# Rearranging the first rounds of a two-layer graph kernel: count reads, a cast, attention logits and a row written to HBM

## The chip, the cores and the metric

The kernel runs on one core of one Trainium2 chip. The metric is device time in microseconds (us) from launch to the end of the kernel. A core has engines that work side by side, each with its own in-order list of instructions: TensorE (PE, matrix products into PSUM), VectorE (DVE), ScalarE (ACT), GpSimd (POOL). SyncE (SP) only issues transfers (DMA), also in order; the transfers themselves run on the core's DMA engines.

## The reference, cut to what matters

The input is a graph of 3327 nodes with 64 features each and a dense 0/1 adjacency matrix. There are two layers, each with a layer norm in front and a residual behind.

```python
# layer 0: attention over hyperbolic log maps
x_t = logmap0(x, c)
left, right = x_t @ w_att[:D, 0], x_t @ w_att[D:, 0]
adj_att = sigmoid(left[:, None] + right[None, :] + b_att[0]) * adj
x_local = logmap(x[:, None, :], x[None, :, :], c)
support_t = einsum('ij,ijd->id', adj_att, x_local)
return proj(expmap(x, support_t, c), c)
...
# layer 1: the last 100 neighbours of each node, weights halving with the rank
rank = cumsum(mask, axis=1); deg = rank[:, -1:]
k = minimum(deg, 100.0); pos = rank - (deg - k)
w = mask * where(pos > 0, 0.5 ** (k - pos), 0.0)
return w @ (input @ weight) + bias
```

Both layers need the adjacency matrix. The kernel reads it once: while layer 0 runs over it, it also counts for each edge how many neighbours lie behind it, and keeps that as small integers for layer 1.

## The kernel before, in words

The nodes are padded to 26 blocks of 128. The output nodes are cut into four strips of 8, 8, 6 and 4 blocks (`STRIPS`), worked in the order blocks 18 to 25, 10 to 17, 4 to 9, 0 to 3. Within a strip, **rounds** go over the 26 source blocks from the last to the first, one block per round in the first three strips and two in the last: 91 rounds in all. A round handles a tile of up to 128 x 1024 pairs.

The work of a round is spread over the engines, and the order of instructions on PE, DVE, ACT and POOL is the order of the program text (`manual_schedule`, line 681). Transfers that SyncE issues are not in that list; their order on the SyncE queue is fixed when the program is built, by the framework. In round n of the loop at line 1173:

- `total` (line 672): PE adds the attention-weighted features of round n-2 into `po`.
- ACT runs two Gelu passes over the pair products `pq` of round n (lines 1190, 1191).
- DVE multiplies the attention by the adjacency (line 1197, the **first product**), which needs the Tanh of round n (line 655) and the adjacency tile `ad`.
- `edges` (line 622): DVE makes the 0/1 mask of round n+3 from its adjacency tile.
- `count` (lines 633, 634): PE adds the mask of round n+2 to running counts in `pc`. There is one `pc` buffer, so a count waits until the one before has been read.
- ACT computes the Tanh of round n+1 (`sigmoids`, line 655).
- `read` (lines 644 to 648): the counts of round n+2 are clipped and written to SBUF, by ACT or by DVE. `ON_ACT` gives the share of ACT, in the first strip every second one, and the first two are always ACT's.
- `products` (lines 662, 663): PE makes the pair products of round n+1. There are two `pq` buffers in PSUM; a new tile waits for the second product of the tile that had its buffer.
- DVE forms the **second product** (line 1214), which needs the Gelu results of round n.

Adjacency tiles have five buffers (`ADB`). The load for round n+4 stands at the head of round n and can start when the first product of round n-1 has let its buffer go.

Before the loop only the node data of blocks 18 to 25 (`first`) are prepared. Those of blocks 0 to 17 (`others`) are made by the generator `second_group`, one step at the end of each of the first rounds, in rounds 0 to 7. Its steps touch: the features `zf` (line 718), a half-precision cast of them on ACT (line 882), the remainder on DVE (line 885), two transposing transfers to `ju` and `jz` (lines 886, 887), logarithms on ACT with their table loads (line 890 and `logarithms`), `artanh` on DVE, and `logits`: 36 small matmuls (line 768) into a tile that takes a turn in the two `pq` buffers, then three DVE instructions (769 to 771). At line 895 the 128 x 18 values of `left` go to an HBM row `left_d`, one 4-byte value at a time; each later strip reads its part of this row, broadcast to 128 partitions, into `left_b` (line 588). While `second_group` still has a step, the loop skips what follows at line 1216, among it the small `range_steps`.

Of the kernel before, what the change touches and what calls it, by code (L numbers as in the profile page):

```python
# [11 lines left out]
F32 = mybir.dt.float32  # L12
# [10 lines left out]
P = 128  # L23
N = 3327
NB = 26
# [5 lines left out]
JD = range(12, 16)  # L31
IN_ORDER = {mybir.EngineType.PE, mybir.EngineType.DVE, mybir.EngineType.Activation, mybir.EngineType.Pool}
AHEAD = 2
SGB, ADB = 5, 5
ON_ACT = ((1, 2), (5, 8), (3, 4), (1, 2))

# [409 lines left out]
def fast(ctx, tc, x, adj_t, r, w_att, b_att, weight, bias, out, flag):  # L446

    nc = tc.nc
# [188 lines left out]
    def read(n, j):  # L637
        k, lo, hi = rounds[n]
        S = strips[k]
        kept = behind(j)[:, S.i0 : S.i0 + S.F]  # L640
        num, den = ON_ACT[k]
        i = NB - 1 - j
        if (n < AHEAD and k == 0) or i * num // den != (i + 1) * num // den:
            A.activation(kept, S.pc[:, : S.F], AF.Relu, scale=128.0 if j in JD else 1.0)  # L644
        elif j in JD:
            V.tensor_scalar(kept, S.pc[:, : S.F], 0.0, 128.0, op0=ALU.max, op1=ALU.mult)
        else:
            V.tensor_scalar(kept, S.pc[:, : S.F], 0.0, None, op0=ALU.max)  # L648
# [16 lines left out]
    def total(n):  # L665
        k, lo, hi = rounds[n]
        S = strips[k]
        if hi == NB:
            S.po = ps.tile([P, FMAX], F32, name="po")
        for j in js(n):  # L670
            for f0, f1 in S.hv:
                T.matmul(S.po[: D + 1, f0:f1], hw[:, j, :], part(n, sg_of[n], j, f0, f1),  # L672
                         start=j == NB - 1, stop=j == 0)
# [23 lines left out]
    zf = d  # L697
# [64 lines left out]

    def logits(bs, tag, bufs):

        plr = ps.tile([P, NB, 2], F32, name=tag, bufs=bufs)
        for b in range(bs.start, bs.stop):
            for part in (0, 1):
                T.matmul(plr[:, b, :], jz[:, b, :], w_h[:, part], start=part == 0, stop=part == 1)
        V.tensor_mul(left[:, bs], plr[:, bs, 0], yr[:, bs])
        V.tensor_mul(right[:, bs], plr[:, bs, 1], yr[:, bs])  # L770
        V.tensor_scalar(right[:, bs], right[:, bs], batt, 0.5, op0=ALU.add, op1=ALU.mult)

    A.activation(load_table, one_c, AF.Ln)
    centred(first)
# [50 lines left out]
    logarithms(first)  # L825
    read(0, NB - 1)
    artanh(first)
    logits(first, "po", 1)
    products(0)
    summing_table(first)  # L830
    pl = first_left()
# [3 lines left out]
    pq = pq_of[0]  # L835
# [11 lines left out]
    def second_group():  # L847

        o = others
        A.activation(rl[:, o], d[:, o], AF.Relu)  # L850
        V.tensor_reduce(ss[:, o], sq2, AX.X, ALU.add)
        V.tensor_scalar(v[:, o], ss[:, o], 1.0 / D, EPS_LN, op0=ALU.mult, op1=ALU.add)
        guess(V, yt[:, o], y[:, o], v[:, o])
        newton(V, yt[:, o], y[:, o], v[:, o], 3)
        A.activation(sr2, rl[:, o], AF.Square)
        yield
        V.tensor_reduce(rs[:, o], sr2, AX.X, ALU.add)
        V.tensor_mul(x2[:, o], y[:, o], y[:, o])
        V.tensor_mul(x2[:, o], x2[:, o], rs[:, o])
        V.tensor_scalar(bal[:, o], x2[:, o], negc, 1.0, op0=ALU.mult, op1=ALU.add)  # L860
        V.scalar_tensor_tensor(babs[:, o], bal[:, o], -1.0, bal[:, o], op0=ALU.mult, op1=ALU.max)
        V.reciprocal(nrm[:, o], babs[:, o])
        V.scalar_tensor_tensor(yz[:, o], nrm[:, o], zs_c, y[:, o], op0=ALU.mult, op1=ALU.mult)

        nz2 = pre.tile([P, n2, D], F32, name="sq2").bitcast(F16).rearrange("p b (c d) -> p b c d", c=2)
        nu2 = pre.tile([P, n2, D], F32, name="sr2").bitcast(F16)
        G.memset(nu2[:, :, KB + 6 :], 0.0)
        G.memset(nu2[:, :, D + 6], -WB * QS)
        G.memset(nu2[:, :, KB + 6], 1.0)
        G.tensor_scalar(as_[:, o], x2[:, o], za_c, None, op0=ALU.mult)  # L870
        the_rest(o, nu2, nu2, KB)
        G.tensor_scalar(x2c[:, o], x2[:, o], MIN_NORM, None, op0=ALU.max)
        t = yt[:, o]
        G.tensor_tensor(yr[:, o], x2c[:, o], nhalf, op=ALU.pow)
        G.tensor_mul(t, yr[:, o], yr[:, o])
        G.tensor_mul(t, t, x2c[:, o])
        G.tensor_scalar(t, t, -0.5, 1.5, op0=ALU.mult, op1=ALU.add)
        G.tensor_mul(yr[:, o], yr[:, o], t)
        clipped(G, o)
        yield  # L880
        features(o)
        A.copy(nz2[:, :, 0], zf[:, o])
        V.tensor_copy(nu2[:, :, :D], zf[:, o])
        yield
        V.tensor_sub(nz2[:, :, 1], zf[:, o], nz2[:, :, 0])
        nc.sync.dma_start_transpose(ju[:, o], nu2.rearrange("p b f -> p (b f)"))
        nc.sync.dma_start_transpose(jz[:, o], nz2.rearrange("p b c d -> p (b c d)"))
        summing_table(o)
        yield
        A.activation(load_table, one_c, AF.Ln)  # L890
        logarithms(o)
        yield
        artanh(o)
        logits(o, "pq", 2)
        nc.sync.dma_start(left_d.rearrange("(b p) -> p b", p=P)[:, o], left[:, o])
        yield
        V.tensor_scalar(balm, bal, MIN_NORM, None, op0=ALU.max)
        V.reciprocal(sk, balm)
        G.tensor_scalar(ih, babs, 2 / WA, None, op0=ALU.mult)
        G.tensor_scalar(w2s, w2, 2.0**27 / HS, None, op0=ALU.mult)  # L900
        G.tensor_mul(su, nrm, balm)
        G.tensor_mul(sv, bal, su)
        G.tensor_scalar(sk, sk, sqc, None, op0=ALU.mult)
        G.tensor_scalar(maxnorm, absr, 1.0 - EPS_BALL, None, op0=ALU.mult)
        G.tensor_mul(c2_c, c_c, c_c)
        G.tensor_scalar(m2c, c_c, -2.0, None, op0=ALU.mult)
        G.tensor_scalar(p2c, c_c, 2.0, None, op0=ALU.mult)
        yield
        ahead.close()

        behind_of["lo"] = ctx.enter_context(tc.tile_pool(name="lo", bufs=1, side="right", reuse_waits="tile")).tile(
            [P, JD.start, NP], U8, name="behind_lo")


    def range_steps():
        t1 = post_pool.tile([P, NB], F32, name="st1")
        V.tensor_mul(t1, nrm, node)
        V.tensor_reduce(st[:, 0:1], t1, AX.X, ALU.max)
        yield 2
        V.scalar_tensor_tensor(t1, x2, c_c, t1, op0=ALU.mult, op1=ALU.mult)  # L920
        V.tensor_reduce(st[:, 1:2], t1, AX.X, ALU.max)
        yield 2
        V.tensor_mul(t1, bal, node)
        V.tensor_reduce(st[:, 2:3], t1, AX.X, ALU.max)
        yield 2
        V.tensor_reduce(st[:, 3:4], t1, AX.X, ALU.min)
        V.tensor_scalar(st[:, 3:4], st[:, 3:4], -1.0, None, op0=ALU.mult)
# [237 lines left out]
    def finish():  # L1165
# [2 lines left out]
                pass  # L1168
        stages.clear()

    stages, rest_of_ahead = [Stage(range_steps())], second_group()
    range_end = in_range()
    for n in range(R):
        k, lo, hi = rounds[n]
        m, w = n + AHEAD, span(n)
        ended, turned = (n > i and rounds[n - i - 1][1] == 0 for i in (1, 2))
        if m + 2 < R:
            if rounds[m + 2][2] == NB:
                strip_in(rounds[m + 2][0])
            load(m + 2)  # L1180
        two = m < R and len(js(m)) == 2
        if two:
            count(m, js(m)[0])
        if turned:
            pa = turn(k - 1)
        elif n > 1:
            total(n - 2)
        pq = pq_of.pop(n)[:, :w]
        if n > 0:
            A.activation(pq, pq, AF.Gelu, scale=-WG / QS)  # L1190
            A.activation(pq, pq, AF.Gelu, scale=WH)  # L1191
        asked_of_act()
        if turned:
            finish()
            stages.append(Stage(per_node(k - 1, pa)))
        sg = sg_of[n][:, :w]
        V.scalar_tensor_tensor(sg, sg, 1.0, ad_of.pop(n)[:, :w], op0=ALU.add, op1=ALU.mult)  # L1197
        if m + 1 < R:
            edges(m + 1)
        if two:  # L1200
            read(m, js(m)[0])
        if m < R:
            count(m, js(m)[-1])
        if n + 1 < R:
            sigmoids(n + 1)
        if m < R:
            read(m, js(m)[-1])
        if ended:
            strip_out(k - 1)
        if 0 < n < R - 1:  # L1210
            products(n + 1)
        if hi - lo > 1:
            advance(PORTIONS[k])
        V.scalar_tensor_tensor(sg, pq, WD, sg, op0=ALU.add, op1=ALU.mult)  # L1214
        if next(rest_of_ahead, True) is None:
            continue
        advance(PORTIONS[k])
        if turned:
            total(n - 2)
        if n > R - 3:  # L1220
            next(range_end)
# [135 lines left out]
```

## Time and profile before

The time before is 434.22 us, the median of three runs (432.78 to 435.92). The profiled execution spans 433.1 us, with a mean granted TensorE clock of 0.956.

| engine | busy us | share of the span |
|---|---|---|
| TensorE (PE) | 369.5 | 85% |
| VectorE (DVE) | 382.3 | 88% |
| ScalarE (ACT) | 364.4 | 84% |
| GpSimd (POOL) | 137.4 | 32% |

The profile is one execution as the hardware profiler records it. Its timeline lists instructions with start, duration, engine and line, and how long the engine had stood idle and for whom. Busy durations of neighbours on one engine overlap a little, so the distance from one start to the next, the pitch, is the better price in a full queue. A round of the first strip costs, by pitch, on DVE 1.13 + 0.62 + 1.13 us (first product, mask, second product) and 1.13 more if DVE reads the counts; on ACT 1.03 + 0.92 + 1.05 us (two Gelu, Tanh) and 0.91 more if ACT reads them.

| first product of round | starts at, us | | round | starts at, us |
|---|---|---|---|---|
| 0 | 25.82 | | 7 | 69.97 |
| 1 | 34.13 | | 8 | 73.14 |
| 2 | 40.06 | | 9 | 80.95 |
| 3 | 46.16 | | 10 | 85.96 |
| 4 | 51.02 | | 11 | 90.23 |
| 5 | 55.03 | | 12 | 93.10 |
| 6 | 62.41 | | 13 | 97.09 |

### The profile page before, as it was taken

How to read it: one execution, taken by the hardware profiler on the slowest of the kernel's cores; microseconds unless marked ns; L12 is line 12 of the kernel's file. 1: busy time of each engine (PE TensorE's matmuls, PEld its weight loads, DVE VectorE, ACT ScalarE, POOL GpSimd, SP SyncE). 2: the span in 40 equal slices, each digit the busy share in tenths (PEclk: the TensorE clock that was granted, in tenths of full speed). 3: DMA queues.
4: the chain of work that ended last, by engine and by line, in shares of the span. 5: the costliest groups of instructions: out<-in, count | busy, mean ns of one | idle time of the engine just before them, and what ended most of it. 6: DMA issues, size and time to landing. Idle time of an engine off the chain costs nothing.

```text
span 433.1 us, 4690 instructions
## 1 busy us (share of the span) xinstructions
PE 369.5 (85%) x1423; PEld 153.1 (35%) x1423; DVE 382.3 (88%) x550; ACT 364.4 (84%) x412; POOL 137.4 (32%) x267
## 2 busy tenths in 40 slices
PE   0485679799999899999999899999787999898883
PEld 0241223233333333333333344444332333343352
DVE  6899976699999989999999898899998999898851
ACT  3495796699999989999999989999897899787620
POOL 6504932000000017581024062850223284253400
PEclk9998888899999999999999899999998999999888
DMA  6612677744455535544444444544543330000012
GB/s 197 179 49 68 155 170 46 196 147 146 145 152 184 169 107 151 177 145 141 123 128 139 145 119 137 148 118 137 173 147 106 110 98 0 0 2 0 1 26 63
DMA packets 32252, 50.28 MB, mean 116 GB/s; under 512 B 17877, under 2 KB 18307, under 8 KB 32218
## 3 DMA queue, kind: packets, MB, share of 16 engines
q1 hardware_dynamic: 29050, 49.07, 40.3%
q10 hardware_dynamic: 2976, 0.75, 0.8%
q8 instruction: 13, 0.21, 0.2%
q14 instruction: 21, 0.17, 0.1%
q0 software_dynamic: 192, 0.07, 0.1%
HBM read 46.40 MB, written 0.86 MB: 109 GB/s over the span
## 4 chain that ended last, share of the span: by engine, by line
DVE 29%; ACT 28%; PE 17%; issue 11%; DMA 10%; POOL 2%; ACTq 0%; POOLq 0%; SPq 0%; DVEq 0%
ACT sg L655 9%; DVE sg L1214 8%; ACT pq L1190 8%; DVE sg L1197 6%; PE po L672 6%; ACT pq L1191 4%; DMA x_sb<-in_x 4%; DMA left_d<-left 3%; ACT behind_lo L644 3%; DMA ad<-in_adj_t 2%; DVE behind_lo L648 2%; DVE wt L1245 2%; ACT behind_hi L644 2%; PE pc L633 2%; PE pq L663 2%
## 5 line engine op out<-in xcount | busy, mean ns | idle before, releaser
L672 PE MATMUL po<-sg,hw 128*65 128x512 f32 (+1 forms) x364 | 167.3, 585 | 0.4 <-DVE st L938 0.4
L1214 DVE SCALAR_TENSOR_TENSOR sg<-pq,sg 128x1024 f32<-128x1024 f32 (+1 forms) x91 | 104.1, 1144 | 9.5 <-ACT pq L1191 9.0
L1197 DVE SCALAR_TENSOR_TENSOR sg<-sg,ad 128x1024 f32<-128x1024 f32 (+1 forms) x91 | 104.7, 1151 | 0.4 <-ACT sg L655 0.3
L655 ACT ACTIVATE sg<-left_b,right 128x1024 f32<-128x1024 f32 (+2 forms) x103 | 99.4, 978 | 0.0
L1190 ACT ACTIVATE pq<-pq 128x1024 f32<-128x1024 f32 (+1 forms) x90 | 86.1, 956 | 8.8 <-PE pq L663 8.4
L1191 ACT ACTIVATE pq<-pq 128x1024 f32<-128x1024 f32 (+1 forms) x90 | 85.2, 946 | 2.9
L633 PE MATMUL pc<-mask,ca 128*128 128x512 bf16 (+1 forms) x175 | 65.1, 372 | 22.4 <-DVE behind_hi L648 7.5
L672 PEld LDWEIGHTS po<-sg,hw 128*65 128x65 f32 x364 | 51.1, 143 | 73.7 <-issue 59.9
L662 PE MATMUL pq<-iu,ju 71*128 71x512 f16 (+1 forms) x182 | 69.7, 383 | 2.2 <-DVE yr L526 0.8
L663 PE MATMUL pq<-iz,jz 128*128 128x512 f16 (+1 forms) x182 | 68.2, 382 | 1.4 <-DMA iz<-nz 1.4
L634 PE MATMUL pc<-mask,cb 128*128 128x512 bf16 (+1 forms) x182 | 66.3, 375 | 1.5 <-DVE sg L1214 1.5
L622 DVE TENSOR_SCALAR mask<-ad 128x1024 bf16<-128x1024 f32 (+1 forms) x91 | 59.5, 654 | 5.1 <-DMA ad<-in_adj_t 5.1
L634 PEld LDWEIGHTS <-cb 128*128 128x128 bf16 x182 | 18.0, 99 | 64.9 <-issue 54.1
L1010 POOL TENSOR_TENSOR dots<-dots,ih 128x8 f32<-128x8 f32 (+1 forms) x3 | 2.6, 873 | 119.3 <-DVE dots L1030 119.3
L1257 PE MATMUL pw<-wt,s 128*128 128x512 bf16 (+1 forms) x154 | 35.6, 388 | 5.1 <-DVE s L1115 2.5
L662 PEld LDWEIGHTS <-ju 71*128 71x128 f16 x182 | 18.3, 100 | 29.2 <-DVE sg L1214 7.9
L633 PEld LDWEIGHTS <-ca 128*128 128x128 bf16 x175 | 17.5, 100 | 30.8 <-issue 19.0
L1257 PEld LDWEIGHTS <-s 128*128 128x128 f16 x182 | 18.4, 103 | 26.1 <-issue 7.1
L1010 POOL TENSOR_SCALAR t<-t 128x8 f32<-128x8 f32 (+1 forms) x9 | 6.3, 702 | 63.7 <-DVE t L1104 63.2
L663 PEld LDWEIGHTS <-jz 128*128 128x128 f16 x182 | 18.4, 101 | 19.2 <-issue 3.4
L644 ACT ACTIVATE behind_lo<-pc 128x1024 uint8<-128x1024 f32 (+2 forms) x29 | 24.9, 858 | 0.0
L644 ACT ACTIVATE behind_hi<-pc 128x1024 uint8<-128x1024 f32 (+2 forms) x24 | 20.7, 863 | 3.4 <-PE pc L634 3.4
(324 smaller groups left out, 389.4 us busy)
## 6 DMA issues: line engine op xcount, KB each, us to landing
ad<-in_adj_t SPq DMA_DIRECT2D x65, 512.0 KB, 3.5
ad<-in_adj_t SPq DMA_DIRECT2D x26, 384.0 KB, 3.1
out<-o SPq DMA_DIRECT2D x6, 128.0 KB, 2.0
x_sb<-in_x ACTq DMA_DIRECT2D x1, 576.0 KB, 15.9
left_b<-left_d SPq DMA_DIRECT2D x1, 512.0 KB
left_b<-left_d SPq DMA_DIRECT2D x1, 384.0 KB
iz<-jz SPq DMA_DIRECT2D x2, 128.0 KB, 2.7
left_b<-left_d SPq DMA_DIRECT2D x1, 256.0 KB
```

Of the source, the lines that this page charges most:

```text
L622: V.tensor_scalar(*args, 0.0, None, op0=ALU.not_equal)
L633: T.matmul(S.pc[:, f0:f1], ca, S.before[:, f0:f1], start=False, stop=True, skip_group_check=True)
L634: T.matmul(S.pc[:, f0:f1], cb, now[:, f0:f1], start=S.first, stop=True, skip_group_check=True)
L644: A.activation(kept, S.pc[:, : S.F], AF.Relu, scale=128.0 if j in JD else 1.0)
L655: A.activation(part(n, sg, j), S.left[:, : S.F], AF.Tanh, bias=right[:, j : j + 1], scale=0.5)
L662: T.matmul(part(n, pq, j, f0, f1), ju[:KB, j, :], S.iu[:, f0:f1], start=True, stop=False)
L663: T.matmul(part(n, pq, j, f0, f1), jz[:, j, :], S.iz[:, f0:f1], start=False, stop=True)
L672: T.matmul(S.po[: D + 1, f0:f1], hw[:, j, :], part(n, sg_of[n], j, f0, f1), start=j == NB - 1, stop=j == 0)
L1190: A.activation(pq, pq, AF.Gelu, scale=-WG / QS)
L1191: A.activation(pq, pq, AF.Gelu, scale=WH)
L1197: V.scalar_tensor_tensor(sg, sg, 1.0, ad_of.pop(n)[:, :w], op0=ALU.add, op1=ALU.mult)
L1214: V.scalar_tensor_tensor(sg, pq, WD, sg, op0=ALU.add, op1=ALU.mult)
```

## The change

The change touches only the first rounds of the first strip. It gives ACT all count reads of rounds 0 to 8 (`EARLY`), so that DVE, which also carries most of `second_group`, has fewer instructions there. It moves the cast of the second group's features on ACT one step later, so that ACT needn't stand waiting for the features, and sends `jz` to its transposing transfer ahead of `ju`. It cuts `logits` of the second group into three pieces that run inside the next rounds: the matmuls near the head of round 6, the three DVE instructions after the first product of round 6, and in round 7 a new piece, which turns `left` into 18 rows of 128 values with a TensorE transpose and a DVE copy, so that `left_d` is written as 18 rows of 512 bytes instead of 2304 single values. The PSUM tile of the logits becomes two banks wide to hold that row and lives from round 6 into round 7. `second_group` has one step more, so `range_steps` starts a round later.

```diff
+EARLY = 9
...
-        if (n < AHEAD and k == 0) or i * num // den != (i + 1) * num // den:
+        if n < EARLY or i * num // den != (i + 1) * num // den:
...
     def logits(bs, tag, bufs):
-        plr = ps.tile([P, NB, 2], F32, name=tag, bufs=bufs)
+        plr = ps.tile([P, 512 + P], F32, name=tag, bufs=bufs)
+        row = plr[:n2, 512:]
+        plr = plr[:, : NB * 2].rearrange("p (b c) -> p b c", c=2)
         for b in range(bs.start, bs.stop):
             for part in (0, 1):
                 T.matmul(plr[:, b, :], jz[:, b, :], w_h[:, part], start=part == 0, stop=part == 1)
+        yield
         V.tensor_mul(left[:, bs], plr[:, bs, 0], yr[:, bs])
         V.tensor_mul(right[:, bs], plr[:, bs, 1], yr[:, bs])
         V.tensor_scalar(right[:, bs], right[:, bs], batt, 0.5, op0=ALU.add, op1=ALU.mult)
+        yield
+        if bs == others:
+            T.transpose(row, left[:, bs], ident)
+            left_t = pre.tile([n2, P], F32, name="left_t")
+            V.tensor_copy(left_t, row)
+            nc.sync.dma_start(left_d.rearrange("(b p) -> b p", p=P)[bs], left_t)
...
         features(o)
-        A.copy(nz2[:, :, 0], zf[:, o])
         V.tensor_copy(nu2[:, :, :D], zf[:, o])
         yield
+        A.copy(nz2[:, :, 0], zf[:, o])
         V.tensor_sub(nz2[:, :, 1], zf[:, o], nz2[:, :, 0])
+        nc.sync.dma_start_transpose(jz[:, o], nz2.rearrange("p b c d -> p (b c d)"))
         nc.sync.dma_start_transpose(ju[:, o], nu2.rearrange("p b f -> p (b f)"))
-        nc.sync.dma_start_transpose(jz[:, o], nz2.rearrange("p b c d -> p (b c d)"))
...
         artanh(o)
-        logits(o, "pq", 2)
-        nc.sync.dma_start(left_d.rearrange("(b p) -> p b", p=P)[:, o], left[:, o])
+        of_others.append(logits(o, "pq", 2))
+        yield
         yield
...
         elif n > 1:
             total(n - 2)
+        for steps in of_others:
+            next(steps, None)
         pq = pq_of.pop(n)[:, :w]
...
         V.scalar_tensor_tensor(sg, sg, 1.0, ad_of.pop(n)[:, :w], op0=ALU.add, op1=ALU.mult)
+        for steps in of_others:
+            next(steps, None)
         if m + 1 < R:
             edges(m + 1)
```

More of the change, by code (lines that the diff above doesn't have):

```diff
@@ L827, in fast @@
     artanh(first)
-    logits(first, "po", 1)
+    for _ in logits(first, "po", 1):
+        pass
     products(0)
@@ L1169, in finish @@
         stages.clear()
+    of_others = []
     stages, rest_of_ahead = [Stage(range_steps())], second_group()
```

## The prediction
> **What bounds the kernel now.** I read the chain of waits first, then the windows by stage, then the waits of the first 90 us, then the timeline of single queues. The chain names a transfer of 9 KB beside the engines. Here is the page's share by line:
>
> ```profile
> ACT sg L655 9%; DVE sg L1214 8%; ACT pq L1190 8%; DVE sg L1197 6%; PE po L672 6%; ACT pq L1191 4%; DMA x_sb<-in_x 4%; DMA left_d<-left 3%; ACT behind_lo L644 3%; DMA ad<-in_adj_t 2%; DVE behind_lo L648 2%; DVE wt L1245 2%; ACT behind_hi L644 2%; PE pc L633 2%; PE pq L663 2%
> ```
>
> No single engine leads it, and `left_d<-left` has 3% of 433 us though it is issued once. The windows (stretch, its length, busy us of PE, PEld, DVE, ACT, POOL, then clock, DMA share, GB/s) show where there is room:
>
> ```profile
> 25.00:60.00 35.00, 22.90 (x66) 7.78 (x65) 31.31 (x46) 28.03 (x33) 17.98 (x29) 0.90 0.49 123
> 60.00:94.00 34.00, 30.00 (x119) 10.98 (x119) 25.36 (x41) 25.33 (x26) 3.10 (x9) 0.85 0.62 119
> 94.00:140.00 46.00, 45.90 (x159) 17.39 (x158) 46.00 (x48) 45.11 (x47) 0.00 (x0) 1.00 0.53 158
> ```
>
> From 94 us on PE, DVE and ACT are all full: a round takes 2.87 or 3.99 us in turn, 3.43 on average, and no time is to be had. From 25 to 94 us none is full. So the change is judged by one question: how much earlier does round 12, at 93.10 us, begin? What comes after is bound by engines at work and should shift as a whole.
>
> The waits of 30 to 90 us (who, for whom, sum, times, longest):
>
> ```profile
> ACT sq L882 <- DVE d L718: 6.7, 1, 6.7
> ...
> ACT pq L1190 <- PE pq L663: 6.1, 3, 3.9
> ...
> DVE mask L622 <- DMA ad<-in_adj_t: 5.1, 2, 3.4
> ...
> PE pq L768 <- DVE sg L1214: 3.2, 1, 3.2
> DVE behind_hi L648 <- PE pc L634: 3.0, 1, 3.0
> ```
>
> ACT stands 6.7 us at the cast of line 882 for features that DVE, then late, makes; PE stands 3.2 us at the logits for their buffer, with `total` of round 4 queued behind; DVE twice lacks an adjacency tile. The SyncE queue tells why:
>
> ```profile
> 62.17 0.39 SPq L895 DMA_DIRECT2D left_d<-left  x1
> 63.65 0.34 SPq L616 DMA_DIRECT2D ad<-in_adj_t  x1
> 77.21 0.33 SPq L588 DMA_DIRECT2D left_b<-left_d  x1
> 77.59 14.21 SPq L616 DMA_DIRECT2D ad<-in_adj_t  x5
> ```
>
> The row is issued at 62.17 and is in HBM some 15 us later, when the read of it at 77.21 may go. The adjacency load issued at 63.65 lands only when the row is done, and the next stands behind the read on the queue. DVE then waits 3.36 us at 77.71 and 1.74 at 83.91.
>
> [...] Here the matmul of 512 columns goes from 0.38 to 0.63 us after the idle stretch of 3.2 us before 60.83, and back at 67.75[...].
>
> **The change part by part.** Pitches as in the table section: DVE round 2.88 us without a read; ACT 3.91 us with one.
>
> (1) Reads. In the first strip odd rounds are ACT's anyway, so the reads of rounds 2, 4, 6, 8 move. They stand in loop rounds 0, 2, 4, 6. DVE loses 4 x 1.13 = 4.5 us, ACT gains 4 x 0.92 = 3.7. Over loop rounds 0 to 6 DVE then has 7 x 2.88 = 20.2 plus the second group, from the timeline 3.8 (30.32 to 34.13), 3.05 (37.01 to 40.06), 2.0, 1.3, 0, 1.7, so 32; ACT has 7 x 3.9 = 27.3 plus two Squares/Relus 2.3, the cast 1.1, the logarithms 3.9, so 34.6. ACT becomes the longer list, and the question is whether it ever waits.
>
> (2) Re-timing the rounds with these pitches. ACT from the Tanh at 28.50: Tanh 1.04, read 0.91, Relu and Square 2.25, then rounds 1, 2 and 3 at 3.91, the cast 1.1 (after the read of round 3, at about 44.4; the features are ready at 43.2, so the 6.7 us wait is gone), round 4 at 3.91, logarithms 3.9, Gelu of round 5 1.95. Sum 26.8, end 55.3. At each step I looked at the producer: counts and products come 1 to 4 us ahead; the clipped values of POOL, which follow `x2` by 12.7 us, come about 50.0, when ACT is at the table load. DVE runs with it: first products at 32.6, 38.9, 43.9, 48.1 and 51.0 for rounds 1 to 5 (before: 34.13, 40.06, 46.16, 51.02, 55.03). In round 5 DVE waits for the Gelu until 55.3 and ends its second product at 56.45 (before: 60.7). **Gain here 4.2 us.** The remainder of line 885 waits nowhere: it follows a second product that ends at 46.75, the cast at 45.5.
>
> (3) Logits. `total` of round 4 now precedes them on PE and needs nothing late. The 36 matmuls still need the buffer that the second product of round 5 frees at 56.45; they take 1.1 us, to 57.6. PE was idle about 2.7 us before that, so its clock may be halved. The three DVE instructions, 0.6 us, need them only after the first product of round 6 (57.6 to 58.75): no wait. But the logits tile now lives until round 7, so the products of round 7 can't take its buffer as they did before (66.95, ahead of the second product at 68.40); they must have that of round 6, free at its second product's end, 61.2.
>
> (4) The row. On DVE the copy stands ahead of the first product of round 7, and waits for the transpose, which on PE stands behind the products of round 7 (0.9 us at full clock, 1.7 at half) and `total` of round 5 (1.75 or 3.4). Neither the transpose nor the copy of 128 columns is in the trace; the nearest rows are the 128-column transposes of line 596 at 0.42 us and the 18-column copies at 0.18. I take 0.4 us for both and the handing over (bounds 0.3 and 0.7). So DVE stands from 61.2 to 64.5 at full clock, or 66.9 at half; I take **65.8**. Behind it wait the first product and the mask of round 10; ACT meanwhile has the Gelu of round 7. The first product of round 7 starts at 65.8, 4.2 us before 69.97. The new stand costs about as much as the old one in round 6 did (DVE 3.0, ACT 3.9).
>
> (5) The transfer. [...] The trace has 3.2 us from issue to landing for another small transfer (`r_c`); I take 2 to 4. It starts at about 66.1 and holds `left_b` and one adjacency load until about 69.5, which then lands 3.5 us later, at 73; its mask is wanted in round 9 at about 74. So the two waits of 5.1 us go. From the first product of round 7: second product and two small instructions to 69.1, round 8 with a DVE read 4.0, so round 9 starts at about 73.1, 7.8 us before 80.95. Before, rounds 9 to 11 took 12.15 us against 2.87 + 3.99 + 2.87 = 9.73 without waits. That adds 2.4: **10.2 us** at round 12.
>
> (6) The SyncE order. `jz` goes first, at 48.1 when the remainder is done, and a transposing issue holds the queue 2.7 us. Whether the load of round 8 stands before or behind it can't be read from the text. Before it: no cost. Behind it: it lands at about 54.5, hidden, since DVE waits for the Gelu until 55.3. Behind it and the two copies that read `jz`: it lands at 57.6 and DVE loses up to 3 us. I take 1 us off. Casts, wider tile, later `range_steps`: no cost; the same instructions in a queue with the same sum.
>
> Sum: 4.2 at round 5, held through round 7, plus about 6.0 from the transfer, less 1: 9.2 us. 434.2 - 9.2 = **425.0 us**.
>
> **Rivals.**
> A, the queue order is bad: adjacency loads behind both transposes. For: the queue is in order, and before the change one load was held at 46.32 to 49.10 by a transpose. Against: the loads had 4 us of slack. Cost 3 in round 5 and 1.2 in round 6 instead of the 1 I took: 428.2.
> B, the stand of DVE in round 7 is at its long end (5.7 us, half clock) and PE then is behind for rounds 8 and 9, as after 60.83, when `total` took 3.65 us. For: PE is idle 2.7 us ahead of the logits and again ahead of the products. Gain 3.1 at round 7, the waits for the transfer (5.1) gone, 2 lost again while the counts lag, 1 at the queue: 5.2 less, of 434.2: 429.0, up to 431.
> C, slower: ACT is the new bound. Its gain of 4.2 at round 5 goes into A's 4.2, the long stand costs 2.5 more than the old one, and the adjacency loads still come late, because the row is issued 4 us later in its round than before and its read still bars the queue: 434.2 + 2.5 = 436.7. For: three new dependences in a row (buffer, transpose, copy). Against: the 15 us write is beyond doubt, and it is gone.
>
> **How the numbers follow.** Forecast 0.55, A 0.20, B 0.17, C 0.08. Range 420.5 to 431.0: the low end has full clock in round 7 (1.3), no cost at the queue (1) and 2 more from PE keeping its clock; the high end takes in A and B and leaves out C. One per cent is 4.3 us. Faster than 429.9: the forecast, nearly all of A, two thirds of B: 0.82. Within 1%: 0.12. Slower: 0.06.
>
> **What would show it.** Right: no wait of ACT for features; the row landing in under 4 us; no wait of a mask for `ad` between 60 and 95 us; the first product of round 12 at 82 to 85 us; unchanged times between rounds after it. A wait of the copy for the transpose of 3 to 5 us should appear in round 7. Wrong: masks that wait for `ad` between 50 and 62 us (A), 0.63 us matmuls through 60 to 72 us (B), a first product of round 9 later than 78 us (C), or a gain at round 12 that a later stage takes back.

## The result and the profile after

The changed kernel takes 428.16 us (median of four runs, 426.61 to 428.44) against 434.14 us before: the ratio is 0.985, with a 95% interval of 0.981 to 0.990. Measured again later, it was 428.94 us with the same ratio, 0.985 (0.982 to 0.989). The forecast was 425.0 us, a gain of 9.2; the gain is 6.0. The time lies inside the range of 420.5 to 431.0. The ratios below leave out one execution, of row6_newton_on_dve (428.35 us), which was over 1.5% longer than the fastest of that kernel.

The profiled execution spans 426.3 us, 6.8 less than before. A line on the chain of waits by share, the answer to the one shown of before:

```profile
DVE sg L1230 9%; ACT sg L656 8%; PE po L673 8%; ACT pq L1204 7%; DVE sg L1211 7%; ACT pq L1205 4%; ACT behind_lo L645 3%; DVE behind_lo L649 2%; DVE wt L1261 2%; PE pq L663 2%; ACT behind_hi L645 2%; PE pq L664 2%; PE pc L634 2%; PE pc L635 2%; PE pw L1273 2%
```

The transfer `left_d<-left` is gone from it; PE's `total` (now line 673) went from 6% to 8%. The stretches (length, busy us of PE, PEld, DVE, ACT, POOL, then clock, DMA share, GB/s):

```profile
25.00:60.00 35.00, 24.41 (x106) 9.27 (x107) 29.62 (x49) 33.35 (x39) 18.32 (x29) 0.92 0.54 136
60.00:86.00 26.00, 23.95 (x71) 8.37 (x72) 20.32 (x32) 22.50 (x23) 3.10 (x9) 0.85 0.43 125
...
94.00:140.00 46.00, 45.63 (x157) 17.25 (x158) 46.00 (x48) 45.23 (x47) 0.00 (x0) 1.00 0.56 169
```

ACT is now full from 25 to 60 us (33.4 of 35, before 28.0), as part (2) of the prediction had it. From 60 us on there are still holes, on DVE most. The waits of 30 to 90 us say where (who, for whom, sum, times, longest):

```profile
DVE left_t L780 <- PE pq L778: 5.5, 1, 5.5
DVE sg L1230 <- ACT pq L1205: 4.7, 2, 4.2
PE pq L771 <- DVE sg L1230: 4.4, 1, 4.4
...
PE pq L663 <- DVE sg L1230: 2.8, 5, 1.5
...
ACT g L750 <- POOL g L745: 1.3, 1, 1.3
```

No mask waits for an adjacency tile any more, and ACT waits for no features. In their place DVE stands 5.5 us for the row's transpose (line 778), and ACT waits 1.3 us for POOL, which the prediction did not have. PE's wait for the buffer of the logits (now line 771) is longer than before, 4.4 us against 3.2. The SyncE queue around the row:

```profile
68.34 0.31 SPq L781 DMA_DIRECT2D left_d<-left_t  x1
69.48 0.34 SPq L617 DMA_DIRECT2D ad<-in_adj_t  x1
69.92 0.38 SPq L589 DMA_DIRECT2D left_b<-left_d  x1
```

The row is issued at 68.34 and its reader goes at 69.92 without a wait, so the row lands within 1.6 us, where it took 15. The profile counts 26757 packets on queue q1 instead of 29050.

The first products (line 1197 before, 1211 after) against the prediction:

| first product of round | before, us | predicted | after |
|---|---|---|---|
| 1 | 34.13 | 32.6 | 32.47 |
| 2 | 40.06 | 38.9 | 38.95 |
| 3 | 46.16 | 43.9 | 43.92 |
| 4 | 51.02 | 48.1 | 48.09 |
| 5 | 55.03 | 51.0 | 51.01 |
| 6 | 62.41 | 57.6 | 59.15 |
| 7 | 69.97 | 65.8 | 68.25 |
| 9 | 80.95 | 73.1 | 75.83 |
| 12 | 93.10 | 82.9 (83.9 with the 1 us for the queue) | 86.52 |
| 90 (last) | 368.84 | | 362.25 |

From round 12 to the last the gain stays what it is, 6.58 and 6.59 us. So in these two traces the gain lies wholly in the first twelve rounds, and I use the first product of round 12 as the ruler for the experiments; it is finer than the times, whose single runs spread over some 2 to 6 us. Two traces of one and the same kernel differ in it too, by 0.3 us (the changed kernel, 86.52 and 86.86), 0.7 (row_in_round6, 82.49 and 83.15) and 1.4 (row6_newton_on_dve, 82.76 and 81.35). Most kernels have a single trace, so half a microsecond on this ruler shows nothing by itself.

### The profile page after: what moved, and what is told of

Its sections match the earlier page's. It is cut to its first block, busy times and chain, and to the rows that moved or that the text cites. A ratio compares the mean times of both kernels' runs of the same rounds, so it can differ in the third digit from the quotient of the medians.

```text
span 426.3 us, 4668 instructions
## 1 busy us (share of the span) xinstructions
PE 365.1 (86%) x1401; PEld 152.7 (36%) x1424; DVE 376.5 (88%) x547; ACT 368.2 (86%) x416; POOL 137.4 (32%) x267
## 3 DMA queue, kind: packets, MB, share of 16 engines
q1 hardware_dynamic: 26757, 49.07, 39.8%
## 4 chain that ended last, share of the span: by engine, by line
DVE 33%; ACT 29%; PE 19%; issue 11%; POOL 5%; DMA 1%; POOLq 0%; SPq 0%; DVEq 0%; ACTq 0%
DVE sg L1230 9%; ACT sg L656 8%; PE po L673 8%; ACT pq L1204 7%; DVE sg L1211 7%; ACT pq L1205 4%; ACT behind_lo L645 3%; DVE behind_lo L649 2%; DVE wt L1261 2%; PE pq L663 2%; ACT behind_hi L645 2%; PE pq L664 2%; PE pc L634 2%; PE pc L635 2%; PE pw L1273 2%
## 5 line engine op out<-in xcount | busy, mean ns | idle before, releaser
L673 PE MATMUL po<-sg,hw 128*65 128x512 f32 (+1 forms) x364 | 164.4, 576 | 0.5 <-DVE st L949 0.4
L634 PE MATMUL pc<-mask,ca 128*128 128x512 bf16 (+1 forms) x169 | 62.8, 372 | 14.9 <-ACT behind_hi L645 4.7
L635 PE MATMUL pc<-mask,cb 128*128 128x512 bf16 (+1 forms) x169 | 61.7, 375 | 2.7 <-DVE sg L1230 1.5
L645 ACT ACTIVATE behind_hi<-pc 128x1024 uint8<-128x1024 f32 (+2 forms) x28 | 24.8, 885 | 4.7 <-PE pc L635 4.7
```

The lines of the kernel that those rows point to most:

```text
L634: T.matmul(S.pc[:, f0:f1], ca, S.before[:, f0:f1], start=False, stop=True, skip_group_check=True)
L635: T.matmul(S.pc[:, f0:f1], cb, now[:, f0:f1], start=S.first, stop=True, skip_group_check=True)
```

## The experiments

All are timed beside the kernel before, in several sessions; the ratio compares within a session, so it says more than two medians of different sessions. "Round 12" is the start of its first product in the profile.

**Undoing the front.** Three kernels take back the reads, the cast, or both, and leave the pieces of the logits and the row.

```diff
 reads_back
-        if n < EARLY or i * num // den != (i + 1) * num // den:
+        if (n < AHEAD and k == 0) or i * num // den != (i + 1) * num // den:
 cast_back
         features(o)
+        A.copy(nz2[:, :, 0], zf[:, o])
         V.tensor_copy(nu2[:, :, :D], zf[:, o])
         yield
-        A.copy(nz2[:, :, 0], zf[:, o])
 both_back: both
```

> The changed kernel with only the reads put back as before: those of rounds 2, 4, 6 and 8 on DVE. Theory of the prediction, DVE is the longer list without the change of reads: DVE has 4.5 us more before round 7, about 3 of it on the path, 431 us. Rival, the reads only swap a DVE bound for an ACT bound, because ACT with all reads is continuously busy to 57 us: within 1 us of the changed kernel, 428.

> The changed kernel with only the cast on ACT put back to the end of round 2 instead of 3. Theory: ACT is free at 40.5 us and waits for the features until 43.2, so all of ACT after it is 2.7 us later; 1.3 us of that fall into the wait for POOL that ACT has at the logarithms anyway, so 1.4 to 2.7 us slower, 430. Rival, the move of the cast is worth nothing once the reads are on ACT: 428.

> The changed kernel with the reads and the cast both put back as before, so that only the pieces of the logits and the row remain of the change. Singly, at the first product of round 12, the reads back cost 1.6 us and the cast back 0.4. Theory: the two stand for each other, since with either one ACT or DVE is relieved enough; together they bring back the old front, in which round 6 starts 3.3 us later than in the changed kernel: round 12 at 89.8, 431.5 us in all. Rival 1, they add up: 2.0 us, round 12 at 88.5. Rival 2, nothing of the front reaches round 12 because the stand for the row takes it up: 86.5.

| kernel | us | ratio to before | round 6 | round 12 | lost at round 12 |
|---|---|---|---|---|---|
| changed kernel | 428.2 | 0.985 | 59.15 | 86.52 | |
| reads_back | 429.5 | 0.991 (0.987 to 0.994) | 60.16 | 88.10 | 1.58 |
| cast_back | 428.0 | 0.990 (0.986 to 0.994) | 60.41 | 86.94 | 0.42 |
| both_back | 431.8 | 0.993 (0.990 to 0.996) | 61.44 | 89.66 | 3.14 |

Reads back costs half of what its theory said, and the cast less than a third: both expectations were too high. The reason shows in the wait of ACT for features, first of cast_back, then of both_back:

```profile
ACT sq L893 <- DVE d L719: 2.6, 1, 2.6
```

```profile
ACT sq L893 <- DVE d L719: 6.4, 1, 6.4
```

With the reads on ACT, DVE reaches the features earlier and ACT the cast later, so that only 2.6 us of the old 6.7 are left to save, and half of these fall into the wait for POOL. Of the 1.3 us that are left at round 6 (60.41 against 59.15), the stand for the row takes up all but 0.4, which is no more than two traces of one kernel differ by. With the cast later, DVE is no longer so urgent. Each edit does most of the other's work; only both back bring the old front again. Round 12 of both_back was expected at 89.8 and is at 89.66; the sum of the two, 88.5, is off by 1.2 us, and so is refuted. The front is worth **3.1 us** on top of the rest.

**The front alone.** The kernel before with `n < 9` in the choice of the reader and the cast a step later, and nothing else of the change.

```diff
-        if (n < AHEAD and k == 0) or i * num // den != (i + 1) * num // den:
+        if n < 9 or i * num // den != (i + 1) * num // den:
 ...
         features(o)
-        A.copy(nz2[:, :, 0], zf[:, o])
         V.tensor_copy(nu2[:, :, :D], zf[:, o])
         yield
+        A.copy(nz2[:, :, 0], zf[:, o])
         V.tensor_sub(nz2[:, :, 1], zf[:, o], nz2[:, :, 0])
```

> The kernel before with only the reads on ACT and the later cast; the logits and the single values as before the change. With the rest alone (both_back) round 12 stood at 89.7, 3.4 us before the old 93.1, and the front had 3.1 on top of it. Theory: the old waits for adjacency tiles follow the row's issue and so move with the front, so that the front gives about 3.1 alone too: round 12 at 90.0, 431. Rival, the freed time is lost in the wait for the 15 us write: round 12 after 91.5.

431.39 us, ratio 0.992 (0.990 to 0.995). Round 12 at 91.18: only 1.9 us earlier than before, against the 3.1 that theory wanted, and nearer to the rival. Its waits of 54 to 92 us hold this one:

```profile
DVE mask L622 <- DMA ad<-in_adj_t: 6.6, 1, 6.6
```

It was 5.1 us in two pieces before. The row is issued 2.5 us earlier, but the rounds come to the missing tile sooner still. The front alone gives 1.9 us and the rest alone 3.4 (93.10 - 89.66), together 5.3 of the 6.6; the 1.2 us that are lacking come only when both are there. That the 15 us write eats them fits the wait for the tile, which is 1.5 us longer, but it is a reading of two traces.

**The price of the single values.** Two kernels do the third piece of `logits` in the middle of round 6, just before the pair products of round 7. One keeps transpose, copy and 18 rows; the other writes the 2304 values one by one.

```diff
 row_in_round6
+        for steps in of_others:
+            next(steps, None)
         if 0 < n < R - 1:
             products(n + 1)
 single_values_round6: the same, and
         if bs == others:
-            T.transpose(row, left[:, bs], ident)
-            left_t = pre.tile([n2, P], F32, name="left_t")
-            V.tensor_copy(left_t, row)
-            nc.sync.dma_start(left_d.rearrange("(b p) -> b p", p=P)[bs], left_t)
+            nc.sync.dma_start(left_d.rearrange("(b p) -> p b", p=P)[:, bs], left[:, bs])
```

> The changed kernel (428.2 us), with the transpose and copy of the row moved from the head of round 7 to the middle of round 6, ahead of the pair products. In the changed kernel DVE stands 5.5 us for that transpose at 62.5 to 68.0 us. Theory: part of that stand is the row's own doing (its place behind the products and the total on PE), but PE works at half clock then and would be late anyway; 2 to 3 us come back, about 425.7, the first product of round 7 starts near 63 instead of 68.25, round 12 near 84 instead of 86.5. Rival 1, the stand is pure loss: 5 us come back, 423. Rival 2, PE's backlog sets the time and the stand hides beside it: 428, no change at round 12.

> As row_in_round6, but the values go to HBM one by one as before the change, without transpose and copy, issued in the middle of round 6. This tells the price of the 2304 small pieces alone, against row_in_round6. Theory: adjacency loads come late again, masks wait 4 to 5 us in rounds 8 to 10, 4 to 5 us slower than row_in_round6, about 430. Rival, the small write lies beside other work and its share of the chain was chance: same as row_in_round6 within 1 us.

Row in round 6: 426.76 us, ratio 0.983 (0.980 to 0.987), round 12 at 82.49. Single values: 430.04 us, ratio 0.992 (0.989 to 0.995), round 12 at 86.68, in a trace whose round 0 begins 0.4 us earlier. Between the two lie 4.6 us at round 12, counted from round 0, and 3.3 us in the medians. The mask waits again with single values:

```profile
DVE mask L623 <- DMA ad<-in_adj_t: 4.6, 2, 3.8
```

That the small write lay beside other work is refuted. And 4.0 us come back at round 12 when the row leaves its place at the head of round 7, between the 2 to 3 of theory and the 5 of the first rival. The next two runs ask what holds these 4.0 us.

No run has the cut of `logits` alone. But single_values_round6 differs from front_alone in little more than that cut and the later issue of the write. Its round 12 is at 86.68 against 91.18, counted from round 0 4.1 us earlier. So, step by step at round 12, the front brings 1.9 us, the cut 4.1 and the 18 rows 4.6, and the place of the row at the head of round 7 takes 4.0 back.

**What the stand in round 7 is made of.** In copy_later only the DVE copy moves, behind the first product of round 7. In own_buffer the row gets a tile of its own, so that the products of round 7 find the logits' buffer free.

```diff
 copy_later
             left_t = pre.tile([n2, P], F32, name="left_t")
+            yield
             V.tensor_copy(left_t, row)
 own_buffer
-        plr = ps.tile([P, 512 + P], F32, name=tag, bufs=bufs)
-        row = plr[:n2, 512:]
+        plr = ps.tile([P, 512], F32, name=tag, bufs=bufs)
 ...
+            row = ps.tile([P, P], F32, name=tag, bufs=bufs)[:n2]
             T.transpose(row, left[:, bs], ident)
```

> The changed kernel with only the DVE copy of the row moved behind the first product of round 7; the transpose stays where it is on PE. DVE then no longer stands with the first product behind the wait. Theory: PE, late and at half clock in its products of round 7 and its total of round 5, sets the time, since the products of round 8 come behind these; DVE's stand is only where the lateness is seen: round 12 at 86.0 to 86.5, 428. Rival, the prediction's step: the stand of DVE is itself on the path: its 4 us come back, round 12 near 82.5 to 83.

> The changed kernel with a tile of its own for the row, so that the buffer of the logits is free after the three small DVE instructions of round 6, and the products of round 7 needn't wait for the second product of round 6. The row's transpose and copy stay at the head of round 7. Theory: the products come 1.4 us earlier (61.2 instead of 62.6), all PE has behind them too, and PE may be at full clock sooner: round 12 1.4 to 3 us earlier, 83.5 to 85.1. Rival, the order on PE (total before the transpose) makes the stand, not the buffer: under 0.5 us.

| kernel | us | ratio to before | round 7 | round 12 | earlier than the changed kernel at round 12 |
|---|---|---|---|---|---|
| copy_later | 426.41 | 0.983 (0.978 to 0.987) | 62.49 | 86.09 | 0.43 |
| own_buffer | 427.98 | 0.984 (0.979 to 0.989) | 66.26 | 84.54 | 1.98 |
| row_in_round6 | 426.76 | 0.983 (0.980 to 0.987) | 62.62 | 82.49 | 4.03 |

In copy_later DVE does its first product of round 7 at 62.49, 5.8 us earlier, and has almost nothing of it five rounds later. The timeline of DVE (start, duration, line, idle time before):

```profile
62.49 1.22 DVE L1212 SCALAR_TENSOR_TENSOR sg<-sg,ad 128x1024 f32<-128x1024 f32 x1
68.18 0.28 DVE L781 COPY left_t<-pq 18x128 f32<-18x128 f32 x1 [4.48 <-PE pq L778]
...
72.82 1.23 DVE L647 TENSOR_SCALAR weight_of<-pc 128x1024 uint16<-128x1024 f32 x1 [0.47 <-PE pc L635]
```

It stands for the same transpose, one instruction later; 4.5 us of the stand are still there. What counts is PE, whose products of round 8, and with them the Gelu of round 8, come behind that transpose in any case. PE has no gap in this trace from 62.63 us to the end of round 8, and DVE's wait for its counts at 72.82, which the changed kernel doesn't have, takes up half of what DVE had gained. PE from the first products of round 7 to the total of round 5, first in the changed kernel:

```profile
62.59 0.61 PE L663 MATMUL pq<-iu,ju 71*128 71x512 f16 x1 [1.47 <-DVE sg L1230]
...
64.27 3.62 PE L673 MATMUL po<-sg,hw 128*65 128x512 f32 x4
...
67.69 0.31 PE L778 MATMUL pq<-ident,left 128*18 128x128 f32 x1
```

in own_buffer:

```profile
60.91 0.63 PE L663 MATMUL pq<-iu,ju 71*128 71x512 f16 x1
...
62.62 3.28 PE L673 MATMUL po<-sg,hw 128*65 128x512 f32 x4
65.74 0.27 PE L778 MATMUL pq<-ident,left 128*18 128x128 f32 x1
```

and in row_in_round6:

```profile
60.82 0.42 PE L778 MATMUL pq<-ident,left 128*18 128x128 f32 x1
...
61.61 0.58 PE L663 MATMUL pq<-iu,ju 71*128 71x512 f16 x1 [0.37 <-DVE left_t L780]
...
62.92 1.88 PE L673 MATMUL po<-sg,hw 128*65 128x512 f32 x4
```

Without the shared buffer PE starts the products at 60.91 instead of 62.59, and round 12 is 2.0 us earlier: the buffer is half of the 4.0 us. The other half, from own_buffer to row_in_round6, holds two things. One is PE's clock: `total` takes 3.28 us in own_buffer, most of it at half clock (a matmul of 512 columns ahead of it took 0.63 us, and takes 0.38 behind it), and 1.88 in row_in_round6; the full clock is back from about 65.5 and from about 62.5 us (67.8 in the changed kernel). The other is DVE's stand, which in own_buffer still is 3.50 us long: from then on DVE has no gap, so its own list sets the time. An estimate from the counts that are read in round 8: PE has them ready at 70.33 us in own_buffer and at 69.12 in row_in_round6, 1.2 later, and DVE reads them at 71.28 and 69.23, which adds 0.8. This split is read from the traces; no run changes the clock alone.

**POOL.** ACT waits 1.3 us for clipped values that POOL makes. The last steps of POOL's list before that, in the kernel before:

```profile
43.04 0.27 POOL L872 TENSOR_SCALAR x2c<-x 128x18 f32<-128x18 f32 x1
43.39 3.26 POOL L874 TENSOR_TENSOR yr<-x2c,nhalf 128x18 f32<-128x18 f32 x1
46.73 0.72 POOL L875 TENSOR_TENSOR yt<-yr 128x18 f32<-128x18 f32 x1
...
49.48 0.20 POOL L744 TENSOR_SCALAR g<-s 128x18 f32<-128x18 f32 x1
```

and after:

```profile
41.94 1.40 POOL L883 TENSOR_SCALAR x2c<-x 128x18 f32<-128x18 f32 x1
43.41 3.70 POOL L885 TENSOR_TENSOR yr<-x2c,nhalf 128x18 f32<-128x18 f32 x1
47.20 1.05 POOL L886 TENSOR_TENSOR yt<-yr 128x18 f32<-128x18 f32 x1
...
50.42 0.23 POOL L743 TENSOR_TENSOR s<-x2c,yr 128x18 f32<-128x18 f32 x1
...
51.12 1.16 POOL L745 TENSOR_SCALAR g<-s 128x18 f32<-128x18 f32 x1
```

DVE beside the last of these:

```profile
46.82 1.34 DVE L896 TENSOR_TENSOR sq<-d,sq 128x1152 f16<-128x1152 f32 x1
...
49.87 1.21 DVE L1230 SCALAR_TENSOR_TENSOR sg<-pq,sg 128x1024 f32<-128x1024 f32 x1
51.01 1.21 DVE L1211 SCALAR_TENSOR_TENSOR sg<-sg,ad 128x1024 f32<-128x1024 f32 x1
```

The same instructions on the same 18 columns take longer: from the list's start (the memset at 38.47 before, at 37.36 after) to the clipped value 11.2 us before, 14.9 after. In both traces, every step between the root (`yr<-x2c,nhalf`) and the clipped value that lasts over 0.5 us begins beside DVE's first product, its `sq<-d,sq` or its mask, and ends 0.06 to 0.09 us after it: after, those at 47.20 (1.05 us, `sq<-d,sq`), 48.32 (1.08, first product), 49.49 (0.55, mask) and 51.12 (1.16, first product); before, those at 46.73 (0.72, first product) and 47.53 (0.55, mask). The one at 50.42 runs beside the second product, which has one of its inputs in PSUM, and takes 0.23 us. So it is less that DVE's list is fuller than which DVE instruction happens to run beside; in the kernel before, too, the step at 49.77, beside `sq<-d,sq`, took 1.46 us. This is read from what runs side by side; no run shifts one of these instructions alone. The test moves this work to DVE:

```diff
 row6_newton_on_dve: row_in_round6, and
-        G.tensor_mul(t, yr[:, o], yr[:, o])
-        G.tensor_mul(t, t, x2c[:, o])
-        G.tensor_scalar(t, t, -0.5, 1.5, op0=ALU.mult, op1=ALU.add)
-        G.tensor_mul(yr[:, o], yr[:, o], t)
-        clipped(G, o)
 ...
         V.tensor_sub(nz2[:, :, 1], zf[:, o], nz2[:, :, 0])
+        V.tensor_mul(t, yr[:, o], yr[:, o])
+        V.tensor_mul(t, t, x2c[:, o])
+        V.tensor_scalar(t, t, -0.5, 1.5, op0=ALU.mult, op1=ALU.add)
+        V.tensor_mul(yr[:, o], yr[:, o], t)
+        clipped(V, o)
```

> row_in_round6 (round 12 at 82.5 us, 426.8 us) with the last four steps of the root and the four clipping instructions of the second group moved from POOL to DVE, at the end of round 3. In the changed kernel and in row_in_round6 ACT waits 1.3 us at the logarithms for the clipped values from POOL. Theory: ACT is the bound there, so everything behind it comes 1.3 us earlier, round 12 at 81.2. Rival: DVE's 1.7 us more in round 3 are on the path instead, or PE's half clock after the logits sets the time: no gain, 82.5 or later.

> row6_newton_on_dve once more, unaltered, which had 424.3 us, with round 12 at 82.8 and none of the loss at the strip changes that both traces of row_in_round6 show. Theory: it is repeatable, 424.3 and no loss there. Rival: it was chance, and this trace loses 1.6 to 2.4 us at the strip changes, 426.

ACT's wait fell to 0.65 us, now for DVE, because one of the eight small DVE instructions took 2.11 us where its neighbours take 0.2:

```profile
49.43 2.11 DVE L745 TENSOR_SCALAR g<-s 128x18 f32<-128x18 f32 x1
49.39 2.12 POOL L739 TENSOR_TENSOR hw<-rl,wn 128x1152 f32<-128x1152 f32 x1
```

It begins 0.04 us after a long POOL instruction and ends 0.03 after it. In the second trace it took 2.11 us again, at 49.00. In the first, then, it is DVE's small instruction that lasts as long as what POOL does beside it, where before it was the other way round. Round 6 comes 0.7 us earlier than in row_in_round6, but round 12 at 82.76 is no earlier than 82.49: the rival was right there. In the second trace it is at 81.35, from a round 0 that began 0.4 us earlier, so 1.0 us better than in the first. The two traces part at PE: DVE waits 1.29 us for the logits in the first and 0.31 in the second. In the second, `total` ahead of them takes 2.68 us, and the matmuls of 512 columns, 0.63 us long before it, take 0.38 from 59.37 on; where PE's clock came back in the first is not shown. What this edit brings at round 12 is not settled. Over the whole kernel it is the best that was run: 424.28 us (median of all six executions, 421.65 to 428.35), ratio 0.974 (0.969 to 0.979), and again 422.20 us, ratio 0.974 (0.970 to 0.979). Beside it, the first time, the changed kernel had 428.94 us, 0.985 (0.982 to 0.989). So it is faster than both kernels.

**Why 4.0 us at round 12 become 1.6 at the end.** In the trace of row_in_round6 the last first product is only 1.6 us ahead of the changed kernel.

> row_in_round6 once more, unaltered. In its first trace 4.0 us gained at round 12 had shrunk to 1.6 at the last round: 1.5 lost at the change from the second to the third strip and 0.9 at the change to the last, each time with a lower granted clock of PE. Theory: where the half clock falls is chance, so a second trace loses another amount or none at these two places, and the mean gain on the changed kernel is between 1.6 and 4 us. Rival: the loss belongs to the kernel, the second trace shows 1.6 again.

> The changed kernel once more, unaltered, beside the next one on the same chip. Expected 428.2 us and the first product of round 12 at 86.5.

The changed kernel repeated its times (428.94 us, round 12 at 86.86). Row_in_round6, again, had 426.25 us, ratio 0.979 (0.976 to 0.983), and a trace with the same two losses: 1.6 us between rounds 50 and 58, 0.9 between 78 and 82. So theory's guess that a second trace would differ fell; the rival was right. Neither trace of row6_newton_on_dve has these two losses: the first leads the changed kernel by 3.8 us at round 12 and at the last round alike. Its advantage over row_in_round6 at the end arises there, at the strip changes, where the edit changes nothing. And four other traces gain 1.65 us at such a place: those of single_values_round6, copy_later, front_alone and the second of row6_newton_on_dve, but not its first; the other ten don't. Copy_later is 0.43 us ahead at round 26 and 2.07 at round 30, where one strip gives way to the next. The stretches there, first the changed kernel, then copy_later:

```profile
140.00:144.00 4.00, 2.33 (x14) 1.28 (x15) 3.72 (x6) 3.69 (x6) 0.00 (x0) 0.86 0.42 131
144.00:148.00 4.00, 4.00 (x9) 1.39 (x8) 4.00 (x5) 3.97 (x5) 0.00 (x0) 0.72 0.41 131
```

```profile
139.60:143.60 4.00, 2.34 (x17) 1.33 (x18) 3.72 (x6) 3.68 (x6) 0.00 (x0) 1.00 0.42 131
143.60:147.60 4.00, 4.00 (x12) 1.31 (x12) 4.00 (x5) 3.97 (x5) 0.00 (x0) 1.00 0.46 131
```

The work is the same, and PE idles the same 1.7 us of four; one kernel gets 0.86 and 0.72 of the clock, the other all of it. What decides between the two was not shown: two traces of row_in_round6 agree, two of row6_newton_on_dve don't. It moves the end by up to 1.7 us at a place, which is a part of the spread of the times. This also hides gains: own_buffer is 2.0 us ahead of the changed kernel at the last round, but its traced execution is only 0.5 us shorter (425.8 against 426.3), so what follows that product took 1.5 us longer; the mean granted clock was 0.95 in it and 0.96 in the changed kernel.

## Why the prediction was right or wrong

**Part (1), the reads, and the pricing of rounds** held: first products of rounds 1 to 5 were met within 0.15 us, and ACT did become the full list. What was not seen is that the reads and the cast of part (2) overlap: singly they are worth 1.6 and 0.4 us, together 3.1.

**Part (2)** has the first failing step: "the clipped values of POOL, which follow `x2` by 12.7 us, come about 50.0, when ACT is at the table load". The one that ACT waits for came at 52.3, as three of POOL's small steps took 1.05 to 1.16 us each beside DVE's `sq<-d,sq` and first products. ACT waited 1.3 us, the Gelu of round 5 ended at 57.0 instead of 55.3, and the gain at the second product of round 5 was 2.5 us instead of 4.2.

**Part (3)** was right in mechanism: the products of round 7 did wait for the second product of round 6, at 62.59, and PE did fall to half clock: 0.50 was granted from 57.6 to 67.6 us. PE stood 4.4 us before the logits where 2.7 were foreseen, because the second product of round 5 came 1.7 us later. How long the half clock lasts, the kernel before showed already: PE worked from 60.83 to 67.75, 6.9 us without a pause, before the full clock was back (0.50 was granted from 60.9 to 67.6), and in own_buffer 7.2 (58.31 to about 65.5).

**Part (4)** named the stand of DVE at 4.6 us (61.2 to 65.8); it was 5.5, near the long end, because PE stayed at half clock for all of the products and the total. Transpose and copy took 0.31 and 0.28 us. The step that failed is whose time this is: "DVE stands ... Behind it wait the first product and the mask". Copy_later shows that to free the first product from the stand brings 0.4 us at round 12 while PE is as late as it is; own_buffer shows that the shared buffer costs 2.0, and row_in_round6 that the row's place costs another 2.0, of which the traces put some 1.2 on PE at half clock and 0.8 on DVE's stand. Nor did "the new stand costs about as much as the old one in round 6": from round 6 to round 7 the lead fell from 3.3 to 1.7 us.

**Part (5)**, the transfer, was right: within 1.6 us where 2 to 4 were taken, the mask waits gone, and the price of the single values 4.6 us by experiment, against 5.1 of waits. Its mis-sized term is the last one, with the sentence of part (6), "Casts, wider tile, later `range_steps`: no cost": rounds 9 to 12 took 10.69 us instead of 9.73, and the steps of `range_steps` that DVE now does in full rounds cost 0.37, 0.31 and 0.27, together 0.95. In the kernel before, such steps were a part of the 12.15 us that I took for waits.

**Part (6)**: the 1 us for the queue was not needed. No load came late. `jz` does not go first, as the prediction and the text on the change have it: `ju` is still issued first, at 44.08, and `jz` at 49.33. In the kernel before, which has the two lines in the old order, SyncE issues them in the same order, at 46.32 and 52.53.

The sum, from 82.9 to 86.5 at round 12: 1.5 at round 6 (POOL 1.3, small things 0.2), 0.9 more by round 7 (half clock), 0.3 to round 9 (the first of the `range_steps`, at 75.53) and 0.95 to round 12 (the others): 3.6. With the 1 us for the queue given back, 2.6 of 9.2 are lost. That 1 us was taken off for a cause that did not occur; it covers a part of the misses by luck. Of the rivals, A did not occur, B occurred in part (half clock in round 7, but PE was back by round 8), C did not. Two of the prediction's own signs of being right failed: round 12 was to begin at 82 to 85 us and the copy to wait 3 to 5 us, and they were 86.5 and 5.5. The other four were met.

## What to carry to other kernels

When a wait is moved, follow who else is behind it: here an engine stood 5.5 us in plain sight, and to let it do one more instruction ahead of the stand brought 0.4, while a shared PSUM buffer and the place of one small transpose and its copy cost 4.0. Two edits that relieve the same pair of engines were not a sum here (1.6 and 0.4 us singly, 3.1 together); undo each alone and both together, and trace the unaltered kernel twice to know how small a difference counts. Price a small transfer by experiment, with what stands behind it in its queue: here 9 KB in 4-byte pieces cost 4.6 us of a kernel whose loads of half a megabyte are hidden.

## What the runs showed that I had not expected

- Small GpSimd instructions on 18 columns took up to five times as long (0.27 and 1.40 us for the same one), not with how full VectorE was, but with which instruction of it ran beside: those that began beside the first product, `d<-rl,yz`, `sq<-d,sq` or the mask lasted until about 0.1 us after its end (0.55 to 1.46 us; one, of 1.70, began beside the first product and lasted until the end of the mask behind it), and those beside one with an input in PSUM took 0.2 to 0.3 us. The other way round, one small VectorE instruction took 2.11 us instead of 0.2 in both traces of row6_newton_on_dve, in the first beside a GpSimd instruction of 2.12.
- TensorE's clock after an idle stretch of 1.85 us (1.86 in copy_later), at the change from the first strip to the second, was 0.86 and then 0.72 over four us each in the changed kernel, and stayed at 1.00 in copy_later. Copy_later gains 1.65 us there on the changed kernel and keeps it to the last round, and so do three other traces, whose clock at this place is not shown.
